# Nine weight loads of 124, each issued as two transfers by rows

## The chip, the cores and the metric

The kernel runs on one core of one Trainium2 chip. The metric is the device time of one execution in microseconds (us); the median of eleven runs is used. One further execution was recorded by the profiler, and all rows of the profile are from it.

The engines are named as in the profile: PE (matmul; PEld its weight loads), DVE (vector), ACT (scalar), POOL (GpSimd) and SP, which here only issues DMA transfers. A core has sixteen DMA engines that move what the queues ask for.

## The reference

The input x has 1024 rows of 32 fields with 128 elements each. For each of the 496 pairs of fields i < j there is a weight matrix W of 128 x 128. The result of a pair is the field i, multiplied by the matrix, times the field j, element by element, in float32:

```python
v_i = inputs[:, I_IDX, :]
v_j = inputs[:, J_IDX, :]
transformed = jnp.einsum('bpd,ped->bpe', v_i, W)
return transformed * v_j
```

The output has 1024 x 496 x 128 float32 values, 260 MB; the weights are 32.5 MB and x is 16.8 MB. The host lays x out with the 128 elements in the partitions (xt) and the weights in groups of four pairs (wt), so that one group is 128 rows of 4 x 128 floats, 2 KB a row and 256 KB in all.

## The kernel before

The pairs are taken in the order of falling i. A pair has two halves of 512 batch rows; a half is one unit u, so there are 992 units, and the work is written out by hand in one loop over u, with no scheduler.

For a unit, `first(u)` issues two matmuls into a PSUM tile `po` and lets ACT scale it (L157 and L158), and `second(u)`, three units later (LAG), issues the third matmul (L166), lets DVE multiply `po` by the field j into the output tile `ot` (L172), and lets SP store it. The three matmuls belong to a split of each float32 operand into three parts [...]: `wh`, `wl`, `wd` for the weights (ACT L94, POOL L95 to L97) and `xh`, `xl`, `xd` for the field i (ACT L109, POOL L110 to L115, or DVE L195). The first fifteen pairs use a plain float32 matmul (L154) while the splits get going.

An output tile holds two pairs: 128 partitions of 2 x 1024 floats, 1 MB, in four buffers. SP stores it with one transfer (L176) as soon as DVE has filled it, 8 KB a row; the last two pairs are stored in halves (L174). DVE can fill a buffer again only when its store has landed.

A weight group of four pairs is loaded by `load_w` (L85) into one of five buffers, four groups ahead of its use (WLEAD). There are 124 groups, numbered c = 0 to 123. Group 0 comes in two pieces by pairs, all others in one transfer. The x fields (L76) are loaded one at a time, 512 KB each, five fields ahead. All of these but four early x loads stand in SP's queue, in the order of the loop: for each group of four pairs one weight load and two stores, and now and then an x load.

`wt[c, :, a:b, :]` is the DRAM side of a weight load and `w_raw[c][:, a:b, :]` the SBUF side, 128 rows on both.

Of the kernel before, what the change touches and what calls it, by code (L numbers as in the profile page):

```python
# [1 line left out]

# [4 lines left out]

F32 = mybir.dt.float32
F32R = mybir.dt.float32r
ALU = mybir.AluOpType  # L10

P = 128
NF = 32
NQ = NF * (NF - 1) // 2
BT = 1024
HB = 512
WC = 2
WL = 4
OG = 2
EPS = 2.0**-12  # L20
NATIVE = 5
SHARED = 10
XDLAG = 10
LAG = 3
WLEAD = 4
XLEAD = 5


def _pairs():

    return [(i, j) for i in range(NF - 2, -1, -1) for j in range(i + 1, NF)]


@with_exitstack
def kernel(
    ctx: ExitStack,
    tc: tile.TileContext,
    xt: bass.AP,
    wt: bass.AP,
    out: bass.AP,  # L40
):

    nc = tc.nc
    pairs = _pairs()
    nchunk = NQ // WC  # L60

    xpool = ctx.enter_context(tc.tile_pool(name="x", bufs=1))
    spool = ctx.enter_context(tc.tile_pool(name="xs", bufs=2))
    rpool = ctx.enter_context(tc.tile_pool(name="wr", bufs=5))
    wpool = ctx.enter_context(tc.tile_pool(name="ws", bufs=4))
    opool = ctx.enter_context(tc.tile_pool(name="o", bufs=4))
    ppool = ctx.enter_context(tc.tile_pool(name="ps", bufs=8, space=bass.MemoryType.PSUM))

    x_sb = {}

    def load_x(f, n=1, pieces=1, eng=None):

        t = xpool.tile([P, n, BT], F32, tag=f"x{f}", name=f"x_{f}")
        s = BT // pieces
        for k in range(pieces):
            (eng or nc.sync).dma_start(out=t[:, :, k * s : (k + 1) * s], in_=xt[:, f : f + n, k * s : (k + 1) * s])  # L76
        for k in range(n):
            x_sb[f + k] = t[:, k, :]

    w_raw = {}  # L80

    def load_w(c, splits=(0, WL)):
        w_raw[c] = rpool.tile([P, WL, P], F32, tag="w", name=f"w_{c}")
        for a, b in zip(splits, splits[1:]):
            nc.sync.dma_start(out=w_raw[c][:, a:b, :], in_=wt[c, :, a:b, :])  # L85

    w_s = {}

    def split_w(c, u):

        k = c * WC % WL
        raw = w_raw[c * WC // WL][:, k : k + WC, :].rearrange("p q e -> p (q e)")
        h, l, d = [wpool.tile([P, WC * P], F32R, tag=t, name=f"{t}_{c}") for t in ("wh", "wl", "wd")]
        nc.scalar.mul(h, raw, 1.0 - 2.0**-13)  # L94
        nc.gpsimd.tensor_tensor(l, raw, h.bitcast(F32), ALU.subtract)  # L95
        nc.gpsimd.tensor_scalar(d, h.bitcast(F32), EPS, 1.0, ALU.mult, ALU.mult)  # L96
        nc.gpsimd.tensor_tensor(d, l.bitcast(F32), d.bitcast(F32), ALU.subtract)  # L97
        w_s[c] = (h, l, d)

    x_s = {}  # L100
    later = []

    def split_x(f, a, u):

        if a == 0:
            x_s[f] = [spool.tile([P, BT], F32R, tag=t, name=f"{t}_{f}") for t in ("xh", "xl", "xd")]
        s = slice(a, a + HB)
        h, l, d = [t[:, s] for t in x_s[f]]
        nc.scalar.mul(h, x_sb[f][:, s], 1.0 - 2.0**-13)  # L109
        nc.gpsimd.tensor_tensor(l, x_sb[f][:, s], h.bitcast(F32), ALU.subtract)  # L110
        nc.gpsimd.tensor_scalar(l, l.bitcast(F32), 1.0 / EPS, 1.0, ALU.mult, ALU.mult)  # L111
        if f > NF - 2 - NATIVE - SHARED:
            later.append((min(u + XDLAG, 2 * first_q[f] + LAG - 1), d, h.bitcast(F32), l.bitcast(F32)))
        else:
            nc.gpsimd.tensor_tensor(d, h.bitcast(F32), l.bitcast(F32), ALU.subtract)  # L115

    nq0 = NATIVE * (NATIVE + 1) // 2
    c0 = nq0 // WC
    first_q = {i: q for q, (i, j) in reversed(list(enumerate(pairs)))}

    todo = []
    for c in range(c0, nchunk):
        todo.append(((c - 3) * WC + 1, max(c * WC, nq0), lambda u, c=c: split_w(c, u)))
    for i in range(NF - 2 - NATIVE, -1, -1):
        for a in range(0, BT, HB):
            todo.append((first_q[i + 1] + 1 if i < NF - 3 - NATIVE else 2, first_q[i], lambda u, i=i, a=a: split_x(i, a, u)))
    todo.sort(key=lambda t: t[1])

    load_w(0, (0, 1, WL))
    load_x(NF - 2, pieces=2, eng=nc.scalar)
    load_x(NF - 1, pieces=2, eng=nc.scalar)
    load_x(NF - 3)
    load_x(NF - 4)
    load_w(1)
    for f in range(NF - 5, NF - 4 - XLEAD, -1):
        load_x(f)
    load_w(2)
    load_w(3)  # L140


    ctx.enter_context(tc.manual_schedule())
    po, ots = {}, {}


    def first(u):
        q, h = divmod(u, 2)
        i, c = pairs[q][0], q // WC
        r = slice(q % WC * P, (q % WC + 1) * P)  # L150
        s = slice(h * HB, (h + 1) * HB)
        po[u] = ppool.tile([P, HB], F32, tag="po", name=f"po_{u}")
        if q < nq0:
            nc.tensor.matmul(po[u], w_raw[q // WL][:, q % WL, :], x_sb[i][:, s], start=True, stop=True)  # L154
        else:
            for t in (0, 1):
                nc.tensor.matmul(po[u], w_s[c][t][:, r], x_s[i][t][:, s], start=t == 0, stop=t == 1)  # L157
            nc.scalar.mul(po[u], po[u], 1.0 + EPS)  # L158

    def second(u):  # L160
        q, h = divmod(u, 2)
        i, j = pairs[q]
        r = slice(q % WC * P, (q % WC + 1) * P)
        s = slice(h * HB, (h + 1) * HB)
        if q >= nq0:
            nc.tensor.matmul(  # L166
                po[u], w_s[q // WC][2][:, r], x_s[i][2][:, s], start=False, stop=True, skip_group_check=True
            )
        g, k = divmod(q, OG)
        if k == 0 and h == 0:  # L170
            ots[g] = opool.tile([P, OG, BT], F32, tag="ot", name=f"ot_{g}")
        nc.vector.tensor_tensor(ots[g][:, k, s], po.pop(u), x_sb[j][:, s], ALU.mult)  # L172
        if q >= NQ - 2:
            nc.sync.dma_start(out=out[g, :, k, s], in_=ots[g][:, k, s])  # L174
        elif k == OG - 1 and h == 1:
            nc.sync.dma_start(out=out[g], in_=ots[g])  # L176

    for u in range(2 * NQ + LAG):
        q = u // 2
        if u % (2 * WL) == 0 and (q // WL + WLEAD) * WL < NQ:  # L180
            load_w(q // WL + WLEAD)
        if u < 2 * NQ:
            i, j = pairs[q]
            if u % 2 == 0 and j == i + 1 and 0 <= i - 2 - XLEAD:
                load_x(i - 2 - XLEAD)
            first(u)
        if u >= LAG:
            second(u - LAG)
        if u % 2 == 1:
            ready = [t for t in todo if t[0] <= q]  # L190
            if ready:
                ready[0][2](u)
                todo.remove(ready[0])
        while later and later[0][0] <= u:
            nc.vector.tensor_tensor(*later.pop(0)[1:], ALU.subtract)  # L195
    assert not todo and not later


# [25 lines left out]
```

## Time and profile before

| | |
|---|---|
| median of 11 runs | 768.68 us |
| lowest and highest | 765.6 and 778.2 us |
| the profiled execution | 768.17 us |
| its span, first to last instruction | 766.4 us |
| PE, DVE, ACT, POOL busy | 94%, 83%, 83%, 77% of the span |
| DMA moved | 310.11 MB, mean 405 GB/s |
| read from and written to HBM | 49.28 and 260.05 MB |
| stores of 1 MB | 247, 8.9 us from issue to landing (median) |
| weight loads of 256 KB | 123, 9.1 us |

The busy share of an engine is an average over the span. A DMA transfer is cut into packets, here one for each row, which the sixteen engines take; a transfer has landed when all engines that took part have said so. The row of the waits names who waited, for whom, how long in all, how often, and the longest time.

### The profile page before, as it was taken

The numbers are of one execution on the slowest core, as the hardware profiler recorded it, in microseconds if no ns is written. First come the engines' busy times: TensorE is split into PE (matmuls) and PEld (weight loads), VectorE is DVE, ScalarE is ACT, GpSimd is POOL, SyncE is SP. The second block draws the span as 40 slices with busy tenths as digits, with TensorE's granted clock in tenths as the row PEclk, the third lists the DMA queues.
The fourth block names the chain that finished last, engine by engine and source line by source line (L and its number), as shares of the span: only waits on it lengthen the run. The fifth ranks groups of instructions, "written<-read, shape, count | busy, mean of one in ns | idle before, by whom it ended". The sixth has DMA issues, their size and how long they took to land.

```text
span 766.4 us, 11824 instructions
## 1 busy us (share of the span) xinstructions
PE 721.9 (94%) x2946; PEld 546.5 (71%) x2946; DVE 632.9 (83%) x1012; ACT 638.2 (83%) x1256; POOL 593.7 (77%) x863
## 2 busy tenths in 40 slices
PE   8978999999999999999999989999999999999994
PEld 3566776767777777777777767777777777777773
DVE  4868988888887788888788878888888888888885
ACT  2277988888988898898888989898989898998983
POOL 2686999888888888878879687978786869696660
PEclk9998999999999999999999999999999999999998
DMA  9999999999999999999999999999999999999997
GB/s 355 425 420 411 419 414 406 399 404 402 417 403 412 412 401 418 406 394 418 409 413 409 402 412 400 412 406 413 413 405 404 403 414 405 406 415 401 402 401 307
DMA packets 59108, 310.11 MB, mean 405 GB/s; under 512 B 6560, under 2 KB 6816, under 8 KB 27424
## 3 DMA queue, kind: packets, MB, share of 16 engines
q1 hardware_dynamic: 58464, 308.31, 99.5%
q10 hardware_dynamic: 576, 1.05, 0.4%
q8 instruction: 24, 0.39, 0.2%
q14 instruction: 44, 0.36, 0.1%
HBM read 49.28 MB, written 260.05 MB: 404 GB/s over the span
## 4 chain that ended last, share of the span: by engine, by line
DMA 50%; PE 29%; DVE 17%; POOL 2%; issue 1%; DVEq 0%; ACT 0%; POOLq 0%
DMA out_dram<-ot 49%; PE po L157 18%; DVE ot L172 16%; PE po L166 9%; PE po L154 2%; DVE xd L195 1%; POOL wl L95 1%; POOL xd L115 1%; DMA x<-in_xt_dram 0%; DVEq L172 0%; POOL wd L97 0%; POOL xl L110 0%; POOL xl L111 0%; ACT po L158 0%; DVEq L217 0%
## 5 line engine op out<-in xcount | busy, mean ns | idle before, releaser
L172 DVE TENSOR_TENSOR ot<-po,x 128x512 f32<-128x512 f32 x992 | 618.8, 684 | 125.2 <-DMA out_dram<-ot 65.2
L158 ACT ACTIVATE po<-po 128x512 f32<-128x512 f32 x962 | 551.0, 582 | 104.3 <-PE po L157 50.9
L157 PE MATMUL po<-xh,wh 128*128 128x512 f32 x962 | 388.2, 404 | 22.6 <-DVE ot L172 19.7
L166 PE MATMUL po<-xd,wd 128*128 128x512 f32 x962 | 376.7, 392 | 5.1 <-DVE xd L195 5.1
L157 PE MATMUL po<-xl,wl 128*128 128x512 f32 x962 | 377.8, 393 | 2.3 <-POOL wl L95 2.2
L157 PEld LDWEIGHTS po<-xh,wh 128*128 128x128 f32 x962 | 180.9, 188 | 105.7 <-DVE ot L172 67.8
L95 POOL TENSOR_TENSOR wl<-w,wh 128x256 fp32r<-128x256 f32 x241 | 179.1, 743 | 89.2 <-ACT wh L94 87.9
L166 PEld LDWEIGHTS po<-xd,wd 128*128 128x128 f32 x962 | 181.2, 188 | 45.9 <-ACT po L158 4.3
L157 PEld LDWEIGHTS po<-xl,wl 128*128 128x128 f32 x962 | 181.3, 188 | 37.8 <-POOL wl L95 5.1
L97 POOL TENSOR_TENSOR wd<-wl,wd 128x256 fp32r<-128x256 f32 x241 | 180.1, 747 | 20.1
L96 POOL TENSOR_SCALAR wd<-wh 128x256 fp32r<-128x256 f32 x241 | 100.0, 415 | 20.3
L94 ACT ACTIVATE wh<-w 128x256 fp32r<-128x256 f32 x241 | 99.1, 412 | 0.5 <-DMA w<-in_wt_dram 0.5
L110 POOL TENSOR_TENSOR xl<-x,xh 128x512 fp32r<-128x512 f32 x52 | 67.2, 1291 | 18.7 <-ACT xh L109 18.4
L115 POOL TENSOR_TENSOR xd<-xh,xl 128x512 fp32r<-128x512 f32 x32 | 41.3, 1292 | 2.7
L109 ACT ACTIVATE xh<-x 128x512 fp32r<-128x512 f32 x52 | 32.4, 627 | 9.7 <-DMA x<-in_xt_dram 9.5
L111 POOL TENSOR_SCALAR xl<-xl 128x512 fp32r<-128x512 f32 x52 | 32.8, 631 | 4.6
L154 PE MATMUL po<-x,w 128*128 128x512 f32 x60 | 28.9, 646 | 3.8 <-DMA x<-in_xt_dram 3.8
L154 PEld LDWEIGHTS po<-x,w 128*128 128x128 f32 x60 | 12.3, 207 | 19.5 <-issue 13.4
L195 DVE TENSOR_TENSOR xd<-xh,xl 128x512 fp32r<-128x512 f32 x20 | 17.2, 862 | 0.0
L109 ACT ACT_TABLE_LOAD x1 | 1.3, 1283 | 2.6 <-issue 2.6
L211 POOL MEMSET const-float32-0.0<- 128x1 f32 x1 | 0.1, 98 | 0.2 <-issue 0.2
L211 POOL MEMSET const-bfloat16-1.0<- 128x1 bf16 x1 | 0.1, 101 | 0.0
(2 smaller groups left out, 0.2 us busy)
## 6 DMA issues: line engine op xcount, KB each, us to landing
out_dram<-ot SPq DMA_DIRECT2D x247, 1024.0 KB, 8.9
w<-in_wt_dram SPq DMA_DIRECT2D x123, 256.0 KB, 9.1
x<-in_xt_dram SPq DMA_DIRECT2D x30, 512.0 KB, 9.1
x<-in_xt_dram ACTq DMA_DIRECT2D x4, 256.0 KB, 4.6
out_dram<-ot SPq DMA_DIRECT2D x4, 256.0 KB, 7.0
w<-in_wt_dram SPq DMA_DIRECT2D x1, 192.0 KB, 3.5
w<-in_wt_dram SPq DMA_DIRECT2D x1, 64.0 KB, 2.8
```

Source lines behind the costliest of these rows:

```text
L94: nc.scalar.mul(h, raw, 1.0 - 2.0**-13)
L95: nc.gpsimd.tensor_tensor(l, raw, h.bitcast(F32), ALU.subtract)
L96: nc.gpsimd.tensor_scalar(d, h.bitcast(F32), EPS, 1.0, ALU.mult, ALU.mult)
L97: nc.gpsimd.tensor_tensor(d, l.bitcast(F32), d.bitcast(F32), ALU.subtract)
L109: nc.scalar.mul(h, x_sb[f][:, s], 1.0 - 2.0**-13)
L110: nc.gpsimd.tensor_tensor(l, x_sb[f][:, s], h.bitcast(F32), ALU.subtract)
L115: nc.gpsimd.tensor_tensor(d, h.bitcast(F32), l.bitcast(F32), ALU.subtract)
L154: nc.tensor.matmul(po[u], w_raw[q // WL][:, q % WL, :], x_sb[i][:, s], start=True, stop=True)
L157: nc.tensor.matmul(po[u], w_s[c][t][:, r], x_s[i][t][:, s], start=t == 0, stop=t == 1)
L158: nc.scalar.mul(po[u], po[u], 1.0 + EPS)
L166: nc.tensor.matmul(po[u], w_s[q // WC][2][:, r], x_s[i][2][:, s], start=False, stop=True, skip_group_check=True)
L172: nc.vector.tensor_tensor(ots[g][:, k, s], po.pop(u), x_sb[j][:, s], ALU.mult)
```

## The change

Nine of the weight loads, those of the groups 11, 25, 39, 53, 67, 81, 95, 109 and 116, are issued as two transfers by rows: eight of them as rows 0 to 123 and 124 to 127, the group 116 as rows 0 to 114 and 115 to 127. All bytes go to the same places as before, and the other loads are untouched.

```diff
+WROWS = {c: 124 for c in range(11, 110, 14)} | {116: 115}
+
     def load_w(c, splits=(0, WL)):
         w_raw[c] = rpool.tile([P, WL, P], F32, tag="w", name=f"w_{c}")
         for a, b in zip(splits, splits[1:]):
-            nc.sync.dma_start(out=w_raw[c][:, a:b, :], in_=wt[c, :, a:b, :])
+            rows = (0, WROWS[c], P) if c in WROWS else (0, P)
+            for r, s in zip(rows, rows[1:]):
+                nc.sync.dma_start(out=w_raw[c][r:s, a:b, :], in_=wt[c, r:s, a:b, :])
```

## The prediction

> **What bounds the kernel now.** I read the busy shares first. No compute engine is full: PE shows 94%, but its matmuls overlap in the record, and DVE and ACT stand at 83%. The DMA row is full from the first slice to the last.
>
> ```profile
> DMA  9999999999999999999999999999999999999997
> GB/s 355 425 420 411 419 414 406 399 404 402 417 403 412 412 401 418 406 394 418 409 413 409 402 412 400 412 406 413 413 405 404 403 414 405 406 415 401 402 401 307
> DMA packets 59108, 310.11 MB, mean 405 GB/s; under 512 B 6560, under 2 KB 6816, under 8 KB 27424
> ...
> q1 hardware_dynamic: 58464, 308.31, 99.5%
> q10 hardware_dynamic: 576, 1.05, 0.4%
> q8 instruction: 24, 0.39, 0.2%
> q14 instruction: 44, 0.36, 0.1%
> ```
>
> q1 is SP's queue: it fills 99.5% of sixteen DMA engines. The rate is 420 to 425 GB/s in the second and third slice and about 405 later, so later something costs 4%. The chain that ended last and the waits tell how the DMA reaches the compute:
>
> ```profile
> DMA 50%; PE 29%; DVE 17%; POOL 2%; issue 1%; DVEq 0%; ACT 0%; POOLq 0%
> DMA out_dram<-ot 49%; PE po L157 18%; DVE ot L172 16%; PE po L166 9%; PE po L154 2%; DVE xd L195 1%; POOL wl L95 1%; POOL xd L115 1%; DMA x<-in_xt_dram 0%; DVEq L172 0%; POOL wd L97 0%; POOL xl L110 0%; POOL xl L111 0%; ACT po L158 0%; DVEq L217 0%
> ```
> ```profile
> DVE ot L172 <- DMA out_dram<-ot: 65.2, 73, 2.6
> DVE ot L172 <- PE po L166: 30.2, 39, 1.4
> ```
> ```profile
> out_dram<-ot SPq DMA_DIRECT2D x247, 1024.0 KB, 8.9
> w<-in_wt_dram SPq DMA_DIRECT2D x123, 256.0 KB, 9.1
> ```
>
> An output of 1 MB takes 8.9 us from issue to landing, but a new one goes out every 2.9 us: it stands in a queue. DVE waits 65.2 us for an output buffer, and a buffer is free only when the last of the transfer's sixteen shares has landed. The trace records when each share landed, without the number of its engine. For the x load issued at 12.2 us all sixteen lie within 0.27 us. For the output issued at 615.0 us the first landed after 4.22 us, the fourteenth 0.28 us later, the fifteenth 0.74 us, **the sixteenth 4.74 us**. From 500 to 740 us nearly every transfer looks so. One DMA engine is late, always by what four output buffers let it be, and fifteen run ahead and are held.
>
> What makes it late is in the packet records. An 8 KB packet takes 309 ns (median), the next on its engine starting 3 to 4 ns before its end. The late engine, followed from 620.8 to 623.1 us, starts its packets 322 ns apart, 16 ns more. It has 247 x 8 = 1976 of them: 1976 x 16 ns = 32 us. Its 2 KB packets start 80.1 ns apart, as elsewhere. An ordinary engine's work is 1976 x 305.5 ns + 1016 x 80 ns (w, and the last outputs) + 240 x 156 ns (x) + about 7 us (small packets) = 729 us, in a DMA stretch from 2.0 to 765.0 us = 763 us. So it has **34 us of slack**, the late engine none. Two other engines are 2 to 4 us behind the median from about 100 to 480 us: they take steps of 1.1 to 1.8 us beside some x loads, and fall back into line when these end. A fetch of PE's instructions (q8, 24 in all) sets its engine back by about 1 us, 24 us in the sum.
>
> **What the Trainium skill says.** "DMA: Bandwidth & Descriptors", section "Why a DMA increments its semaphore by 16 and not by 1": a transfer runs on the largest k up to 16 that divides the slowest dimension of both sides, and from SP's queue on the lowest-numbered k engines. 128 rows give 16, which the trace bears out (16 landings each); 124 and 4 give 4, 115 gives 5, 13 gives 13; no run here shows these yet. The same page, "Latency and other measured facts", says that engines 7 and 15 are usually slower than the rest, with a guess at a cause that is not this queue's. The trace agrees that one engine is slow, not which. The same page, "Rules for kernel authors", advises one 128-row transfer in place of two, since two share the same engines; with k = 4 that reason falls away.
>
> **The change, part by part.** It is nine loads, not eight: range(11, 110, 14) has eight values, and 116 is the ninth. Nothing of the computation moves, and SP alone gets rows: nine DMAs.
> - *Packets moved.* A w load is 128 packets of 2 KB, 8 an engine. As 124 + 4 rows it is 31 + 1 = 32 on engines 0 to 3 and none on 4 to 15. As 115 + 13 it is 23 + 1 on 0 to 3, 24 on 4, 1 on 5 to 12, none on 13 to 15. Sum: engines 0 to 3 get 8 x 24 + 16 = +208 packets; 4 gets -64 + 16 = -48; 5 to 12 get -71; 13 to 15 get -72. At 80.1 ns: **+16.7 us, -3.9, -5.7, -5.8 us**.
> - *On the path.* The late engine never rests, so what leaves it leaves the time: 5.7 to 5.8 us if it is one of 5 to 15. The +16.7 us on 0 to 3 is covered by their 34 us of slack. Between two such loads lie 14 w loads, 81 us, in which an ordinary engine has 81 x 34/763 = 3.6 us of slack, for 24 x 80.1 ns = 1.9 us. At the moment itself an engine that runs 4.5 us ahead stays 2.6 us ahead. If that cover is gone (an engine of 0 to 3 is late itself), the whole 16.7 us less its slack is paid.
> - *Issue.* Nine more issues on SP, 0.33 us each at the least (row L176's shortest): 3 us of SP, which waits 466 us for DVE's products; cost nothing. The outputs and x loads behind them go out at most 0.5 us later, into queues some 4 us deep. The second piece waits for nothing new but its own landing semaphore, free since the transfer eight places earlier; eight places last some 15.5 us, now 13.5 around a split load, against 8.9 to landing. Completion packets: 9 ns each, fewer on most engines.
> - *Landing of the split loads.* Four engines take 2.6 us where sixteen took 0.65, but need not wait for the late one (4.7 us). ACT's L94 takes a load up 11 pairs (16 us) after its issue at the earliest, and waited 0.5 us for w in all. Zero.
> - *Unseen cost:* 32 packets queued at once on one engine, and four engines writing rows outside their usual share. Bounds: from 0 to the 2 us by which such a load is longer, nine times 2 = 18 us if all queues stopped behind it. I take 0.3 us in the sum, since 4 us of queue stand before the late engine.
>
> Sum: -5.8 + 0.3 = -5.5 us. The profiled execution took 768.17 us (span 766.4 and 1.8 around it), 0.5 below the median of 768.68. So 762.7 on that execution, **763.2 on the median**. DVE's waits for the outputs should then fall from 65 to about 60 us; next late are PE's products (L166, 30 us) and the two other lagging engines.
>
> **Rivals.**
> 1. *A lagging engine among 0 to 3.* The two that fall behind beside x loads come within 0.02 to 2 us of the last one before 480 us; with five of the split loads by then, one of them pays 5 x 1.9 = 9.6 us less 2 of slack, and the slow engine later gives back four loads' 4 x 0.64 = 2.6: about +5 us, 773. PE's fetch engine has 34 - 24 = 10 us of slack for 16.7, so +6.7, 775; if a fetch of 16 KB costs it only the bytes (two 8 KB packets, 0.61 us, 15 us in all), -2.3, 766. For it: of sixteen engines three lag so, and the trace gives no numbers. Against it: other places are three times as many for each.
> 2. *The slow engine is itself one of 0 to 3.* Then +16.7 us goes straight on the path: 785, **slower**. It decides from the point at which an engine of 0 to 3 has less than 10.9 us of slack (16.7 less 5.8). For it: nothing in the trace excludes it. Against it: the skill's 7 and 15, and 12 places of 16.
> 3. *The split runs on all engines after all.* Then it is nine DMAs with 16 completion packets of 9 ns each: +1.3 us at most, 769 to 770, no change.
>
> **How the numbers follow.** About 0.5% (3.8 us) is what a measurement of this kernel can tell from no change. Forecast 0.50, 761.5 to 764.7, almost all faster. Rival 1: 0.29, three quarters of it within the bound. Rival 2: 0.14. Rival 3 and mishaps of issue: 0.07, mostly no change. Faster 0.48, same 0.30, slower 0.22. The range takes the forecast, rival 3 and most of rival 1: 761 to 773.5; it leaves out rival 2 and little else. Across the forecast alone it would be 761.5 to 764.7.
>
> **What would show it.** Right: DVE's wait for outputs near 60 us, w rows of 248 KB and 8 KB in the issues with landings shorter than 9.1 us, the sixteenth share of an output still 4 to 5 us behind the first. Wrong: outputs landing in more than 8.9 us with a larger wait of DVE on them (rival 1 or 2; in 2 the last share falls 2 us further back at each split load), or w pieces landing with sixteen shares (rival 3).

## The result: slower by 1.1%, and the profile after

The changed kernel takes 776.28 us (median of 12 runs, 773.52 to 783.51), the kernel before 768.26 us (median of all its runs beside it). The ratio is 1.0111, with a 95% interval of 1.0085 to 1.0137: 8.5 us lost (6.5 to 10.5). The prediction had 763.2 us, at most 773.5. The profiled execution took 779.41 us, with a span of 777.5. Ratios, here and below, leave out slow executions, those more than 1.5% above the fastest of the same kernel (three of the 47 of before, five of the fourteen of add_0, two of the four of add_01, one each of probe_before and four_of_nine).

The page of the kernel after, its DMA rows (one value for each fortieth of the span in the GB/s row; then packets by queue with the share of sixteen engines' time):

```profile
GB/s 351 424 420 385 412 417 404 392 402 401 406 413 394 392 385 419 396 377 405 413 386 381 397 412 417 393 372 411 417 395 391 416 420 410 372 418 393 406 411 327
DMA packets 59046, 310.11 MB, mean 399 GB/s; under 512 B 6498, under 2 KB 6754, under 8 KB 27362
...
q1 hardware_dynamic: 58402, 308.31, 98.4%
```

The bytes are the same, but the rate now has dips (385, 392, 377, 381, 372) that the row of before does not have, and the queue's share fell from 99.5% to 98.4%: engines stand idle for lack of packets. The count of small packets shows on how many engines the split loads run. Each engine that takes part adds one completion packet: 401 whole transfers x 16 + 8 x (4 + 4) + (5 + 13) = 6498, the number in the row. This is what the Trainium skill says in "DMA: Bandwidth & Descriptors", section "Why a DMA increments its semaphore by 16 and not by 1" (the largest divisor up to 16); the trace agrees to the packet. That these are the lowest-numbered engines is taken from there too: the trace gives no numbers of engines, so every number below rests on it.

The waits of the kernel after (who waited, for whom: us in all, times, longest), and its DMA issues:

```profile
DVE ot L178 <- DMA out_dram<-ot: 91.6, 98, 4.0
...
PE po L163 <- DVE ot L178: 36.3, 39, 3.5
DVE ot L178 <- PE po L172: 17.0, 25, 1.4
```
```profile
w<-in_wt_dram SPq DMA_DIRECT2D x8, 248.0 KB
...
w<-in_wt_dram SPq DMA_DIRECT2D x1, 230.0 KB
```

All line numbers stand six higher than before. DVE's wait for a free output buffer, forecast at 60 us, went from 65.2 to 91.6 us, and PE, held up in its turn by DVE, waits 36.3 us at L163, where it had waited 19.7:

```profile
PE po L157 <- DVE ot L172: 19.7, 29, 1.4
```

DVE's wait for PE's last product, the next in size, fell from 30.2 to 17.0. This is the sign that the prediction named for rivals 1 and 2.

One split load shows how. Busy time by stretch of the span, from 496 to 499 us and from 506 to 512 us (the last three columns are the granted PE clock, the share of the DMA engines and GB/s): first the kernel before, then the kernel after, where the load of group 81 was issued at 492.8 us.

```profile
496.00:499.00 3.00, 2.69 (x13) 1.88 (x12) 2.51 (x5) 2.36 (x5) 2.28 (x4) 1.00 1.01 421
506.00:512.00 6.00, 6.00 (x26) 4.62 (x26) 5.18 (x9) 5.63 (x13) 4.44 (x7) 1.00 1.02 420
```
```profile
496.00:499.00 3.00, 3.00 (x15) 2.48 (x14) 2.38 (x5) 2.79 (x6) 2.75 (x5) 1.00 0.76 309
506.00:512.00 6.00, 4.17 (x11) 3.30 (x12) 4.75 (x8) 2.11 (x5) 1.88 (x4) 0.72 0.83 343
```

From 496.3 to 497.3 us only six to eight packets are under way at a time, where sixteen engines could move one each: most engines without a share of the load have run dry, and the rate from 496 to 499 us is 309 in place of 421 GB/s. The load's four shares land at 500.3, 500.4, 502.9 and 504.2 us. Of the output issued behind it at 495.7 us the median share lands at 500.2, the fifteenth 5.2 and the sixteenth 6.4 us later, so that it lands 10.9 us after its issue and not 8.9. DVE then waits for the buffer (3.0 us, until 507.1), and from 509.2 to 510.4 us only four or five packets are under way. Two of the engines 0 to 3 had been the last two already when the load came; now they are further back.

**The last engine is another one.** The trace gives the time of each share of a transfer. The time from the sixteenth share of one transfer to the sixteenth of an output that follows it is the last engine's step for an output, 8 packets of 8 KB. In before its median is 2578 ns (200 to 450 us) and 2588 ns (450 to 740 us): the engine with the slow packets. In after it is 2466 and 2471 ns, eight packets at the ordinary 308 ns. An ordinary engine, loaded by the split loads, has become the last one. Until 140 us the step of after is still the slow engine's (2578 ns from 20 to 80 us, 2588 from 80 to 140); the second split load is issued at 145 us. This step serves as a fingerprint of the engine that binds in the experiments.

### The profile page after: what moved, and what is told of

Read it like the earlier page. It is cut to its first block, busy times and chain, and to the rows that moved or that the text cites. A ratio compares the mean times of both kernels' runs of the same rounds, so it can differ in the third digit from the quotient of the medians.

```text
span 777.5 us, 11851 instructions
## 1 busy us (share of the span) xinstructions
PE 715.1 (92%) x2946; PEld 549.3 (71%) x2946; DVE 632.8 (81%) x1012; ACT 633.3 (81%) x1256; POOL 595.1 (77%) x863
## 2 busy tenths in 40 slices
DMA packets 59046, 310.11 MB, mean 399 GB/s; under 512 B 6498, under 2 KB 6754, under 8 KB 27362
## 3 DMA queue, kind: packets, MB, share of 16 engines
q1 hardware_dynamic: 58402, 308.31, 98.4%
## 4 chain that ended last, share of the span: by engine, by line
DMA 44%; PE 35%; DVE 15%; issue 2%; POOL 2%; SPq 0%; DVEq 0%; POOLq 0%
DMA out_dram<-ot 44%; PE po L163 23%; DVE ot L178 13%; PE po L172 11%; DVE xd L201 2%; PE po L160 1%; POOL xd L121 1%; DMA x<-in_xt_dram 1%; POOL wl L101 0%; SPq L91 0%; DVEq L178 0%; POOL wd L103 0%; POOL xl L116 0%; POOL wd L102 0%; POOL xl L117 0%
## 5 line engine op out<-in xcount | busy, mean ns | idle before, releaser
L178 DVE TENSOR_TENSOR ot<-po,x 128x512 f32<-128x512 f32 x992 | 619.1, 684 | 136.4 <-DMA out_dram<-ot 91.6
L163 PE MATMUL po<-xh,wh 128*128 128x512 f32 x962 | 386.7, 402 | 37.3 <-DVE ot L178 36.3
L163 PE MATMUL po<-xl,wl 128*128 128x512 f32 x962 | 378.5, 393 | 6.2 <-POOL wl L101 6.2
L163 PEld LDWEIGHTS po<-xh,wh 128*128 128x128 f32 x962 | 181.7, 189 | 109.7 <-DVE ot L178 71.4
L163 PEld LDWEIGHTS po<-xl,wl 128*128 128x128 f32 x962 | 182.1, 189 | 42.2 <-POOL wl L101 8.6
L115 ACT ACTIVATE xh<-x 128x512 fp32r<-128x512 f32 x52 | 32.6, 630 | 10.5 <-DMA x<-in_xt_dram 10.4
L160 PEld LDWEIGHTS po<-x,w 128*128 128x128 f32 x60 | 12.2, 207 | 20.3 <-issue 13.5
```

## The experiments

My theory after the result was that engines 0 to 3 got more work than they had slack (**work**). Against it stood: the second transfer on SP costs (**issue**); 2.6 us of packets at once on four engines cost, however much slack there is (**burst**); and the late engine is itself one of 0 to 3 (rival 2). The table gives the packets that an engine got more or less, in us at 80.1 ns for 2 KB (61 ns for the 1.5 KB of add_0123), the ratio to the kernel before with its interval, and the last engine's step in the two stretches.

| kernel | engines 0–3 | engines 4–15 | ratio | step, ns |
|---|---|---|---|---|
| before | | | 1 | 2578, 2588 |
| after | +16.7 | -3.9 to -5.8 | 1.0111 (1.0085–1.0137) | 2466, 2471 |
| even_nine | 0 | 0 | 1.0020 (1.0003–1.0036) | 2576, 2586 |
| half_burst | +16.7 | 4–14 -5.1, 15 -10.3 | 1.0106 (1.0069–1.0144) | 2464, 2463 |
| double_124 | +34.6 | -11.5 | 1.0292 (1.0263–1.0321) | 2459, 2458 |
| add_0123 | +15.9 | 0 | 1.0101 (1.0078–1.0124) | 2464, 2466 |
| four_of_nine | +7.7 | -2.6 | 0.9982 (0.9966–0.9998) | 2472, 2474 |
| relieve_7 | 0–6 +6.4 | 7–8 -4.5, 9–15 -5.1 | 1.0091 (1.0061–1.0120) | 2574, 2584 |
| relieve_15 | 0–7 +1.0 | 8–14 0, 15 -7.7 | 1.0026 (1.0006–1.0047) | 2530, 2585 |
| relieve_9_15 | 0–1 +4.5, 2–8 +3.8 | 9–15 -5.1 | 1.0055 (1.0040–1.0069) | 2467, 2496 |

All kernels that split loads have this edit, with their own `CUTS`:

```diff
-            nc.sync.dma_start(out=w_raw[c][:, a:b, :], in_=wt[c, :, a:b, :])
+            rows = (0, *CUTS.get(c, ()), P)
+            for r, s in zip(rows, rows[1:]):
+                nc.sync.dma_start(out=w_raw[c][r:s, a:b, :], in_=wt[c, r:s, a:b, :])
```

**Is it the second transfer?** The same nine loads, cut where both pieces run on sixteen engines:

```diff
+CUTS = {c: (112,) for c in (*range(11, 110, 14), 116)}
```

> The same nine weight loads in two transfers, but of 112 + 16 rows, so that every DMA engine gets 7 + 1 packets, as many as before. Theory 'work' (two of the engines 0 to 3 had some 5 us of slack, not 34, and the changed kernel gives them 16.7 us more; the time is the sum of the work on the fullest engine): 768 us, no change. Theory 'issue' (a second transfer holds SP's queue, and what stands behind it starts late): 774 to 777 us, as the changed kernel. Theory 'burst' (32 packets at once on four engines are more than four output buffers can ride out, whatever the sum): 768 us.

Measured: 1.0020, 1.5 us for nine more transfers, 0.17 us each. The page's issues show both pieces landing like any load (median us in the last column):

```profile
w<-in_wt_dram SPq DMA_DIRECT2D x9, 224.0 KB, 9.8
...
w<-in_wt_dram SPq DMA_DIRECT2D x9, 32.0 KB, 9.1
```

The slow engine is still the last (2576, 2586). Issue explains 1.5 of 8.5 us (0.2 to 2.8 by the interval).

**Is it the burst?** The same 16.7 us on engines 0 to 3, in sixteen loads of 68 + 60 rows in place of nine, each a smaller step:

```diff
+CUTS = {c: (68,) for c in range(8, 120, 7)}
```

> Sixteen loads of 68 + 60 rows: engines 0 to 3 get 17 + 4 = 21 packets in place of 8, 16 x 13 = 208 more in the sum, as in the changed kernel, but in steps of 1.04 us and not of 1.92; engines 4 to 14 get 4, engine 15 none. 'Work': 208 packets of 80.1 ns are 16.7 us as in the changed kernel, so 774 to 779 us. 'Burst': a step of half the size is ridden out, 766 to 770 us. 'Issue': sixteen second transfers for nine, 782 us.

Measured: 1.0106, as in after. The loss does not fall with the size of the step, so burst, which had 766 to 770 us, is out, and so is issue with 782; the dips at the split loads are where the loss shows, not why it arises.

**Twice the split loads:**

```diff
+CUTS = {c: (124,) for c in range(8, 116, 6)}
```

> Eighteen loads of 124 + 4 rows: engines 0 to 3 get 18 x 24 = 432 packets more, 34.6 us. 'Work': the first 5 us are hidden, the rest shows: 768 + 30 = 798 us, over three times the step of the changed kernel (8 us) for about twice the loads. 'Burst' and 'issue': a price for each load, 18/9 x 8 = +16, 784 us.

Measured: 1.0292, 22.4 us for +34.6. That is between the two expectations, 784 and 798 us, and decides for neither. It is more than twice the loss of after, as work less a fixed slack gives, but the slack is not one number: 34.6 less 22.4 is 12.2 us, against 16.7 less 8.5, 8.2 us.

**Is the relief of engines 4 to 15 worth anything?** The loads stay whole, and nine further loads of 116 rows of 1.5 KB, whose tile nobody reads, run on engines 0 to 3:

```diff
+    qpool = ctx.enter_context(tc.tile_pool(name="ex", bufs=1))
...
+            if q // WL + WLEAD in (*range(11, 110, 14), 116):
+                t = qpool.tile([P, 3, P], F32, tag="extra", name=f"extra_{q}")
+                nc.sync.dma_start(out=t[:116], in_=wt[q // WL + WLEAD, :116, :3])
```

> The same nine extra loads with 116 rows: 15.9 us each on engines 0 to 3. 'Work': as the 58 rows, 775 to 776 us, for engines 1 and 3 are alike. 'Pairs': 780 to 782 us. It is the changed kernel's load on 0 to 3 without its relief of 4 to 15, so the difference to 776 us is what that relief is worth.

Measured: 1.0101, with the same last step as after. Load on 0 to 3 alone, with nothing taken from the others, gives the whole loss, within the intervals; that 4 to 15 are relieved buys nothing to be seen once an engine of 0 to 3 is the last. 'Pairs', the idea of the next two expectations that engine 1 shares something with engine 9 and so gained from its relief in after, had 780 to 782 us for this kernel; its median is 774.17. The waits of this kernel (L174 is the line of DVE's product here) look like those of after:

```profile
DVE ot L174 <- DMA out_dram<-ot: 87.4, 87, 4.0
```

The same on engine 0 alone (29 rows) and on 0 and 1 (58 rows):

> The kernel before with nine loads more, of 29 rows of 1.5 KB into a tile that nobody reads, at the places of the nine split loads: 261 packets of 61 ns, 15.9 us, on engine 0 alone, and no engine relieved. If engine 0 has 16 us of slack, as the tiny loads in the changed kernel suggest (it stood among the early ones): 768 to 769 us. If all of the engines 0 to 3 are equally near the limit: 775 us or more.

> The same nine extra loads with 58 rows: 15.9 us each on engines 0 and 1. Engine 1 was the last one of the changed kernel. 'Work', each engine on its own: engine 1 has the slack that the changed kernel showed (16.7 - 8 = 8 to 9 us), so +7, 775 us. 'Pairs' (engine 1 and the late engine 9 share something, so that relieving 9 also helped 1): nothing is relieved here, so only some 4 us are hidden, +12, 780 us.

Measured: 1.0068 (1.0026–1.0109) and, from two executions only, 1.0133 (1.0067–1.0199). This did not tell the engines apart. The fourteen times of the first lie in two groups, 768.0 to 771.4 (five) and 775.3 to 783.5 (nine); its profiled execution, 769.36 us, shows no loss to speak of. Whether engine 0 alone binds stays open.

**Which engines are the last?** Sixty loads of 16 bytes a row were added, of 17 to 119 rows and 8 to 15, which run on the lowest 1 to 15 engines; the shares of each tell whether the late ones are among them.

> The kernel before, with 60 tiny loads (16 bytes a row, into a tile that nobody reads), one behind every second weight load, of 17, 34, 51, 68, 85, 102, 119, 8, 9, 10 to 15 rows in turn. 17 rows run on engine 0 alone, 34 on 0 and 1, and so on up to 15, so that the landings of each tiny load, set beside the sixteen landings of the weight load ahead of it, tell how late each numbered engine is. Time within 1% of 768 us. Theory 'work': the last engine (slow packets) is one of 4 to 14, and two of the engines 0 to 3 lag by 2 to 4 us while x loads run. Rival 'slow engine among 0 to 3': the last share is in the set of every tiny load on 0 to 3, and the time of the changed kernel is its 16.7 us, less what it wins back when the others rest.

> The changed kernel with the same tiny loads. Both theories: the two last shares are engines of 0 to 3; the numbers say whether they are the two that lag in the kernel before ('work') or the slow engine and another ('slow engine among 0 to 3'). Time within 1% of 776 us.

Measured: the probes cost some 0.13 us each in before (1.0099) and 0.17 in after (786.70 us in place of 776.28, ratio to before 1.0256, more than the 1% that was expected), so these are not quite the kernels they look into. In the changed kernel the load on two engines (34 rows) has, from 200 us on, one share 2.6 to 3.9 us behind the other: engine 1. The load on three has still one late share, the load on four a second: engine 3. For example, at 436.2 us the four shares land 0.1, 0.2, 3.3 and 4.0 us behind the median of the load ahead. Engines 0 and 2 stand in line with the rest, so of the four with equal packets two have slack and two have none. In the kernel before no probe on one to four engines has a share more than 1.2 us late, so the two that lag beside x loads are not among 0 to 3 there, though that had been expected; none on up to nine has one more than 3.0 us late. After 300 us the load on ten has one of 3.8 to 4.3 us, the load on eleven still one as late, and the load on twelve two, so there the late two are engines 9 and 11. That is at odds with what follows.

**Where does the slow engine sit?** Five kernels bear on it. 120 + 8 rows take 7.7 us from engine 15 alone, 63 + 63 + 2 rows take 5.1 us from 9 to 15, 119 + 9 rows 4.5 us from 7 and 8 as well:

```diff
+CUTS = {c: (120,) for c in range(11, 111, 9)}
```
```diff
+CUTS = {c: (63, 126) for c in range(11, 120, 14)}
```
```diff
+CUTS = {c: (119,) for c in range(11, 110, 14)}
```

> Twelve loads of 120 + 8 rows: engine 15 gets none of them (96 packets less, 7.7 us), engines 0 to 7 one packet more each (1 us), the others 8 as before. If the engine with the slow packets is number 15: the next ones are some 5 us behind it, so 763 us (762 to 765). If it is another: 768 to 769 us. 'Issue': twelve second transfers cost 12/9 x 8 = 11 us, 779 us.

> Eight loads in pieces of 63 + 63 + 2 rows: engines 9 to 15 get none of them (64 packets less, 5.1 us), 2 to 8 get 14 packets in place of 8 (48 more, 3.8 us), 0 and 1 get 15 (56 more, 4.5 us). The tiny loads put the two last engines of the kernel before at 9 and 11. 'Work' and 'pairs': these are 5.1 us earlier, and engine 1 stays inside its slack, so 763 to 765 us. If engine 1 has less than 5 us: 767 to 769. 'Issue': sixteen transfers more than before, 775 or more.

> Eight loads as 119 + 9 rows: engines 0 to 6 get +80 packets (6.4 us), engines 7 and 8 get -56 (-4.5 us), 9 to 15 get -64 (-5.1 us). If the engine that is late in the kernel before is 7 or 8 and the others have 8 us or more of slack: faster by up to 4.5 us less about 1.2 us for eight more transfers, ratio 0.995 to 0.998. If it is one of 4 to 6 (or 0 to 3): slower by 6.4 us, ratio 1.008 to 1.010. If the late engine is not the same in every execution: in between, 1.001 to 1.006.

Measured: 1.0026, 1.0055 and 1.0091. None gains. In relieve_7 the slow engine is the last one throughout (2574, 2584 ns), and the loss of 7.0 us is the 6.4 us that engines 0 to 6 got, about the whole of it: what is laid on the engine without slack goes straight into the time. So it is not 7 or higher. In four_of_nine, below, 0 to 3 got 7.7 us and nothing was lost, so it isn't one of 0 to 3. That leaves 4 to 6. The skill's remark in "Latency and other measured facts" of the same page, that 7 and 15 are usually slower, finds no support here: in relieve_7 both were relieved, and the slow engine was still the last. The reasoning takes it that the same engine is slow in every execution. Relieve_7 and four_of_nine ran on one chip, but the others on three more, and two of these speak against it. In probe_before the steps are 2496 and 2504 ns, and the late engines 9 and 11. In relieve_9_15 an engine of 4 to 6 got 3.8 us and should have stayed the last; yet the last one is ordinary (2467 and 2496 ns), as if the slow one were among the relieved 9 to 15. So the place is inferred and not shown.

The loss of relieve_9_15, 4.2 us, was not foreseen either (763 to 769 us were expected under work, 775 under issue; 771.46 was measured). Sixteen more transfers at 0.17 us are an estimated 2.7 us of it. The other 1.5 us leave the engine that binds there, which got 3.8 to 4.5 us, a slack of only 2 to 3 us. Which engine that is stays open.

**Work within the slack.** If engines 0 to 3 have some 8 to 10 us, four split loads fit:

```diff
+CUTS = {c: (124,) for c in (25, 53, 81, 109)}
```

> Four of the loads as 124 + 4 rows (groups 25, 53, 81, 109), the others whole: engines 0 to 3 get +96 packets (7.7 us), engines 4 to 15 get -32 (-2.6 us). Slack theory (engines 0 to 3 have some 8 to 10 us to give, a late engine of 4 to 15 gets 2.6 us back): ratio 0.997 to 1.000, 766 to 768 us. A price for each such load in its place (8 us for nine, so 0.9 us each, whatever slack is left): 1.0046, 772 us. Work that goes straight on the path from the first packet: +7.7 us, 1.010.

Measured: 765.45 us (22 runs), ratio 0.9982 (0.9966–0.9998), 1.4 us faster than before (0.2 to 2.6). A price for each load would have made it slower by 3.5 us, work straight on the path by 7.7. It is the fastest of all kernels here, if barely. The last engine is already an ordinary one (2472, 2474 ns). It fits that the slow one was relieved of 2.6 us and stepped back, and that what 0 to 3 had is about used up; which engine is the last was not probed here.

## Why the prediction was wrong

- **Where the packets go: right.** Nine loads, 4 + 4 and 5 + 13 engines, +208 packets on 0 to 3; the count of completion packets agrees exactly.
- **What the late engine gives back: right in kind.** Four_of_nine gains 1.4 us of the 2.6 less some 0.7 for four more transfers. In after this gain is out of sight, since the end is set elsewhere.
- **"The +16.7 us on 0 to 3 is covered by their 34 us of slack": this is the step that failed.** Given and lost: 16.7 and 8.5 us (after), 15.9 and 7.8 (add_0123), 16.7 and 8.1 (half_burst), 34.6 and 22.4 (double_124), 7.7 and -1.4 (four_of_nine). So the weakest engine of 0 to 3 has some 8 to 12 us, not 34. (Relieve_9_15, where nine engines got more, leaves even less to one of 0 to 8.)
- **The term that was mis-sized** is the 729 us of an ordinary engine. It was a sum of packet counts and *median* times. In before the 8 KB packets have a median of 309 but a mean of 319.0 ns, those of 4 KB 159 and 168.9, those of 2 KB 84 and 85.8. The excess of all packets over the medians is 384 us, 24 us for each engine on the mean, the slow engine's 32 being only a small part of it. With about 23 us more, an ordinary engine works 752 us of 763 and has 11 us left. How the excess falls on single engines the trace doesn't tell. Fetches of instructions come on top for those that carry them. The page said so without any packet record: q1 takes 99.5% of 766.4 us, 762.6 us an engine, of which some 12 us are counted twice because packets overlap by 3 to 4 ns; that is 751 us of 763 on the mean. The prediction quoted this row and then worked with 729.
- **Rival 1 came about**, in its second form: it had 34 less 24, 10 us of slack, for the engine with PE's fetches and gave 775 us. The size is right, and the last engines of the changed kernel are two of 0 to 3. But the 10 us came out right by luck: the 34 were 23 too many, and the 24 us of PE's fetches that were taken off are another thing. That PE's fetches are the reason was not shown: in after the last engine's steps exceed the ordinary ones by about 0.3 us on the mean where one of the other fetches (q14) lies in them, but by no more than 0.1 where one of PE's does, as where none does. Most of the 24 us of excess are long packets of outputs, x and weights.
- **Rival 2** (785 us) did not happen: with the slow engine among 0 to 3 it would have stayed the last in after, and four_of_nine would have lost its 7.7 us. **Rival 3** is excluded by the packet count.
- **Issue: said to cost nothing, costs a little.** 0.33 us an issue at the least was expected; the two pieces of group 81 took 1.3 and 1.5 us, and the output behind them 1.0. Even_nine puts a second transfer at 0.17 us, 1.5 us in all, where the sum had 0 and 0.3 for unseen costs.
- **Landing of the split loads: no cost, as said.** They land 11.4 us after issue (median of the nine first pieces), where less than 9.1 had been named as a sign of being right, but ACT still waits only 0.5 us for w in all.
- **DVE's wait as a sign** is rough: even_nine, 1.5 us slower, shows 74.1 us, four_of_nine, 1.4 us faster, 77.3, and relieve_7, 7.0 us slower, 66.7, against 65.2 in before. The last engine's step told the cases apart, the wait did not.

## What to carry to other kernels

Before work is moved onto a shared engine "with slack", take the slack from its busy share, or from mean packet times, not from counts times the median: a tail of a few per cent, 3% of the mean here, was 24 us of 763 and two thirds of the slack. A transfer whose rows don't divide by 16 ran on fewer engines here; moving work so could pay only up to the slack of the weakest of them, and then cost nearly microsecond for microsecond (from after to double_124, 17.9 us more work and 13.9 us more time). Four such loads were worth 1.4 us, nine cost 8.5.

## What had not been expected of the hardware

- In the changed kernel engines 0 to 3 got the same packets, and yet two of them (1 and 3 by the probes) ran 3 to 5 us behind while the other two kept with the rest.
- 8 KB packets come in a normal length of 309 ns, with 1% of them at or above 606 ns, twice as long; single packets of 2 KB last up to 1.7 us, of 4 KB up to 1.2 (all in before). What lengthens them was not tried.
- Which engine is the last changes with a load of a few microseconds: with +7.7 us on four engines and -2.6 on the others the slow one is no longer last. With its queue at 99.5%, this kernel was bound by one DMA engine and, but for some 10 us, by others too.
